# A decoder layer on one core: transposing x and x1 by VectorE blocks and DRAM instead of TensorE, and a new order for the first batch

## The chip, the cores and the metric

The kernel runs on one core of one Trainium2 chip. The metric is the device time of one execution in microseconds. The engines are called PE (TensorE), DVE (VectorE), ACT (ScalarE), POOL (GpSimd) and SP (SyncE, which here only issues DMAs). PEld is PE's weight load.

## The reference

There are 16 batches of 512 tokens with 256 channels, all in float32. One post-norm decoder layer is computed: a linear attention, a cross-attention on 64 context tokens per batch, and a mixture of 8 experts with a capacity of 1024 tokens each.

```python
x = layernorm(x + attn(x))          # q = x + x Wq + bq; two products of K^T V, 16 heads of 16
x = layernorm(x + xattn(x, ctx))    # 16 heads of 64, softmax over 64 context tokens
x = layernorm(x + ffn(x))           # router softmax, first 1024 tokens of each expert

# attn, for k in (0, 1):
states[k] = (x + x Wk[k] + bk[k])^T (x + x Wv[k] + bv[k])   # per head, scaled by 1/1024
out = q @ (states[0] * states[1])
out = layernorm(out) * ln_g + ln_b
out = out @ Wo + bo
```

Nearly all router weights are above zero, so each expert's first 1024 tokens are those of batches 0 and 1; the kernel works these two out beside the attention and has a loop at the end for whatever else would be routed.

## The kernel before

The self-attention never forms keys and values of tokens. For each batch it takes the Gram matrix of x (`gram`, L550 to L576: `gx` is x with a column of ones), and turns it with the weights into the state (`g_times_wk`, `states`) and into a 256 x 264 matrix `m`. The tokens then go through `m` (L687), a norm, the output projection (L711) and the norm that gives `x1`. A matmul contracts over partitions, so tokens that are to be multiplied have to lie with their channels on partitions. That is what `transposed` (L227 to L241) does: eight 128 x 128 transposes on PE (L233) into two PSUM banks, then one copy of each bank to SBUF. It is called for x (`xT`, L664), for x1 (`x1T`, L723), for the two batches of the experts and for weights and context in the setup. `zT` (L696 to L703) is transposed likewise and shares its buffer with `xT`. In `x1T` the tokens are put in another order (token 128 t + 32 q + i goes to column 32 t + i of block q), and its last row is set to one, so that the mask can be added as a row of the keys.

The cross-attention of a batch has four tiles of scores (L814), a softmax on DVE, ACT and POOL whose end is a transpose in blocks of 32 x 32 on DVE (`probsT`, L804), and then 256 matmuls in one go (L834) on the values already multiplied by the output weights (`vo`), which come from DRAM by SP's DMAs (L781). The experts' matmuls are L946 and L963.

The order of all instructions is settled when the program is built. Each part is a stream, a Python generator that yields between small steps. `Model` keeps an estimate of when each engine is free and each tile made; `weave` takes, of the streams that are ready, the one whose own clock is least. A stream's clock is `at + span * spent / total`, set by `plan`: how much of PE's time it has spent of its total, spread over its span. `yield WAIT` makes a stream wait until the estimate says that its last step is done, and `beside` runs a generator as a further stream. The setup is planned to last 115 us and each batch a STEP of 78 us. The plan of before has the self-attention of batch b from SETUP + (b - 1) STEP (L1071) and its cross-attention one STEP later (L1084); the experts are a stream over nearly the whole run (L1117). `in_order` then fixes the order on PE, DVE, ACT and POOL. Each engine works its list in order; all DMAs are issued from SP, in order too, and one that waits holds those behind it.

The lines that are spoken of: L186 and L188 (`evac`, copies on ACT and DVE in turn), L237 and L239 (the copies to `x1T`), L267 (a norm on ACT), L296 and L299 (`load_gram_x`: a memset on POOL and the load of `gx`), L426 (loads of context weights, `nat`), L611 (load of `xt`), L725 (POOL adds a bias to x1), L822 (exponentials), L870 (store of `x_rest`), L952 and L954 (relu of `hT`).

Of the kernel before, what the change touches and what calls it, by code (L numbers as in the profile page):

```python
# [18 lines left out]
P = 128  # L19
# [8 lines left out]
class Model:  # L28
# [37 lines left out]
    def run(self):  # L66
# [4 lines left out]
        for ins in traced[self.seen:]:  # L71
# [12 lines left out]
            if kind == "InstDMACopy":  # L84
# [13 lines left out]
            for n in names[0] + names[1]:  # L98
                self.used[n] = max(self.used.get(n, (0.0, None)), (done, engine), key=lambda p: p[0])
            for n in names[1]:  # L100
                self.made[n] = (done, engine)
# [15 lines left out]
def decoder_layer(  # L117
# [93 lines left out]

    not_last = const.tile([P, 1], FP, tag="not_last", name="not_last")
# [6 lines left out]
    w_sel = const.tile([P, NTT, E], FP, tag="w_sel", name="w_sel")  # L219
# [7 lines left out]
    def transposed(dst, src, view=lambda t: t, ones=False):  # L227


        for cc in range(NC):  # L230
# [4 lines left out]
            ps = ps if len(v.shape) == 2 else ps.rearrange("p (q t i) -> p q t i", q=NT, t=NT)  # L235
            if ones and cc == NC - 1:
                nc.vector.tensor_scalar(v, ps, not_last, ident[:, P - 1:P], ALU.mult, ALU.add)  # L237
            elif ones:
                nc.scalar.copy(v, ps)  # L239
            else:  # L240
                evac(v, ps)  # L241

# [29 lines left out]
    with ExitStack() as att:  # L272
# [20 lines left out]
        def load_gram_x(b, eng=nc.sync, pieces=1):  # L293
# [4 lines left out]
            for i in range(pieces):  # L298
                eng.dma_start(  # L299
                    out=t[:, i * n_:(i + 1) * n_, :C],  # L300
                    in_=x[b, i * n_ * P:(i + 1) * n_ * P, :].rearrange("(t p) c -> p t c", p=P),
                )
# [147 lines left out]
        def context_keys():  # L450
# [28 lines left out]
            last = small.tile([P, NP], FP, tag="last", name="last")  # L479
# [70 lines left out]
        def gram(b, u4):  # L550
# [12 lines left out]
            if b + 2 < B:  # L563
                gram_x[b + 2] = load_gram_x(b + 2)
# [10 lines left out]
            grams[b] = g  # L575
            yield WAIT  # L576
# [30 lines left out]
        grams, sums = {}, {}  # L607
# [6 lines left out]
        def self_attention(b, done):  # L614
# [4 lines left out]
            xT = wk1.tile([P, NC, S], FP, tag="xT", name="xT")  # L619
            gks = []  # L620
# [42 lines left out]
            yield from until(lambda: made(xt))  # L663
            transposed(xT, xt)  # L664
# [16 lines left out]
            yield WAIT  # L681
            z = wk1.tile([P, NT, CX], FP, tag="z", name="z")
            mm = moments()
            for t in range(NT):
                ps = bank("ps_o")
                for cc in range(NC):
                    nc.tensor.matmul(  # L687
                        ps[:, :CX], xT[:, cc, t * P:(t + 1) * P], m[:, cc, :], start=(cc == 0), stop=(cc == NC - 1)
# [19 lines left out]
            for t in range(NT):  # L708
# [7 lines left out]
                yield  # L716
            yield from until(lambda: finished["routing"] >= b - 1)
# [3 lines left out]
            x1T = wk2.tile([P, NC, S], FP, tag="x1T", name="x1T")  # L721

            transposed(x1T, x1, lambda t: t.rearrange("p (t q i) -> p q t i", q=NT, t=NT), ones=True)  # L723
            yield WAIT
            nc.gpsimd.tensor_add(x1, x1, cs["bout"].unsqueeze(1).to_broadcast([P, NT, CX]))  # L725
            done[b] = x1, x1T

# [37 lines left out]
        def cross_attention(b, x1, x1T):  # L765
# [41 lines left out]
            for t in range(NT):  # L807
# [3 lines left out]
                for hf in range(2):  # L811
                    ps = bank("ps_sim")
                    for cc in range(NC):
                        nc.tensor.matmul(  # L814
                            ps, x1T[:, cc, t * P:(t + 1) * P], kq[:, cc, hf * 512:(hf + 1) * 512],
# [59 lines left out]
        def ranks():  # L875
# [34 lines left out]
            nc.vector.scalar_tensor_tensor(w_sel, rank, float(CAP), w_all, ALU.is_lt, ALU.mult)  # L910
            NB = B - HEAD_B
            least = small.tile([P, NB], FP, tag="least", name="least")
# [9 lines left out]
        def last_norm(b, t):  # L922
            y = wk1.tile([P, C], FP, tag=("z", "xt")[t % 2], name="y")
# [120 lines left out]
        done, finished = {}, {"states": 0, "cross": 0, "routing": 0}  # L1044
# [24 lines left out]
        def all_self_attention():  # L1069
            for b in range(B):  # L1070
                self_st.plan(SETUP + (b - 1) * STEP, STEP, 16.5)  # L1071
                yield from until(lambda: b in grams and sums[b // QB][1] and "rb" in cs and made(grams[b], sums[b // QB][1][0]))
# [9 lines left out]
        def all_cross_attention():  # L1082
            for b in range(B):
                cross_st.plan(SETUP + b * STEP, STEP, 28.2 + (0 if b % GB else 4.0))  # L1084
# [33 lines left out]
        self_st.plan(0.0, SETUP, 16.5)  # L1118
        cross_st.plan(SETUP, STEP, 28.0)
# [40 lines left out]
    with tc.For_i(0, n, 1) as i:  # L1160
# [3 lines left out]
        nc.vector.tensor_copy(wb, w_sel[:, ds(i * NT + HEAD_B * NT, NT), :])  # L1164
# [47 lines left out]
```

## Time and profile before

| what | value |
|---|---|
| three runs | 1383.49, 1384.72, 1386.94 us, median 1384.72 |
| the profiled execution | 1389.4 us, of which its span is 1387.6 |
| busy: PE, DVE, ACT, POOL | 1365.9, 850.7, 402.2, 203.7 us |
| granted PE clock, mean | 0.994 |
| moved by DMA | 153.6 MB, 40.1% of 16 engines' span on SP's queue |
| groups of transposes at L233 | xt 128, x 128, nat 32, cn 16, x_head 16 |

The profile's page gives the busy time of each engine, the chain of waits that ended last, the groups of instructions with the mean length of one, and the DMA issues with the time from issue to landing. Of the further views, the windows give the busy time of each engine in a stretch, and the timeline gives the instructions with start, length and the idle time before them (in brackets, with what ended it). Times within the run are in us from the start of the span. Matmuls are pipelined, so the lengths of neighbours overlap, and the distance between starts is what one costs.

### The profile page before, as it was taken

Reading aid. Unit: us, or ns where it says so; the run is one execution under the profiler, and the core shown is the slowest. Engines: PE = TensorE matmul, PEld = TensorE weight load, DVE = VectorE, ACT = ScalarE, POOL = GpSimd, SP = SyncE. Lnnn points to the kernel's source line nnn. Section 1 sums busy time; section 2 is a strip of 40 time slices with the busy share of each in tenths; the row PEclk is TensorE's granted clock in tenths of the full one; section 3 lists DMA queues with packets and bytes.
Section 4 is the critical chain, followed back from the end, with each engine's and each line's share of the span. In section 5 each row is a group of like instructions: output and inputs, shape, how many; then the busy total and the mean of one; then the engine's idle time right before and its main releaser. Section 6 shows DMA issues by size and latency. Waiting matters only on the chain.

```text
span 1387.6 us, 24209 instructions
## 1 busy us (share of the span) xinstructions
PE 1365.9 (98%) x9630; PEld 1077.9 (78%) x9630; DVE 850.7 (61%) x1957; ACT 402.2 (29%) x912; POOL 203.7 (15%) x140
## 2 busy tenths in 40 slices
PE   8999999999999999999999999999999999999997
PEld 5766576877878787878878787878888787878686
DVE  2445848466584848475584848475665939484744
ACT  1134224132232314142233323142323323232322
POOL 0001112112020111112020112112020202111200
PEclk9999999999999999999999999999999999999999
DMA  8657775511515153522606053513334061505211
GB/s 260 203 136 191 189 195 163 142 32 42 145 53 150 46 142 106 127 77 52 181 24 164 31 142 106 126 62 77 110 95 123 16 187 46 147 26 126 91 56 40
DMA packets 98372, 153.57 MB, mean 111 GB/s; under 512 B 15560, under 2 KB 70096, under 8 KB 98256
## 3 DMA queue, kind: packets, MB, share of 16 engines
q1 hardware_dynamic: 98256, 151.98, 40.1%
q8 instruction: 78, 1.28, 0.4%
q14 instruction: 38, 0.31, 0.1%
HBM read 114.71 MB, written 37.22 MB: 109 GB/s over the span
## 4 chain that ended last, share of the span: by engine, by line
PE 89%; DVE 5%; DMA 2%; SPq 1%; ACT 1%; issue 1%; ACTq 0%; DVEq 0%
PE ps_x L834 16%; PE ps_sim L814 15%; PE ps_e L963 15%; PE ps_h L946 15%; PE ps_gk L629 4%; PE ps_p L711 4%; PE ps_o L687 3%; PE ps_kv L437 3%; PE ps_t L233 2%; PE ps_kq L751 2%; PE ps_vo L492 2%; PE ps_s L641 2%; PE ps_g L555 2%; PE ps_zt L700 1%; PE ps_m L670 1%; PE ps_g L560 1%
## 5 line engine op out<-in xcount | busy, mean ns | idle before, releaser
L946 PE MATMUL ps_h<-head_T,wi 128*128 128x256 f32 x1024 | 239.1, 379 | 0.0
L834 PE MATMUL ps_x<-vo,pT 32*128 32x264 f32 x4096 | 234.9, 384 | 3.9 <-DVE pT L804 3.7
L814 PE MATMUL ps_sim<-kq,x1T 128*128 128x512 f32 x512 | 235.0, 593 | 0.0
L834 PEld LDWEIGHTS ps_x<-vo,pT 32*128 32x128 f32 x4096 | 211.5, 186 | 26.1 <-issue 5.6
L946 PEld LDWEIGHTS ps_h<-head_T,wi 128*128 128x128 f32 x1024 | 193.4, 190 | 38.8 <-issue 13.0
L802 POOL TENSOR_TENSOR s<-s,sm 128x1024 f32<-128x1024 f32 x64 | 121.7, 1901 | 539.8 <-DVE sm L801 501.4
L841 DVE TENSOR_TENSOR x<-ps_x,x 128x264 f32<-128x264 f32 x64 | 23.2, 426 | 226.3 <-PE ps_x L834 226.3
L822 ACT ACTIVATE s<-s 128x512 f32<-128x512 f32 x128 | 80.7, 630 | 276.1 <-DVE s L821 276.0
L814 PEld LDWEIGHTS ps_sim<-kq,x1T 128*128 128x128 f32 x512 | 94.5, 190 | 83.2 <-issue 74.5
L820 DVE TENSOR_REDUCE mx<-ps_sim 128x8 f32<-128x512 f32 x128 | 86.1, 673 | 42.0 <-PE ps_sim L814 41.6
L821 DVE TENSOR_TENSOR s<-ps_sim,mx 128x512 f32<-128x512 f32 x128 | 88.5, 692 | 4.4
L725 POOL TENSOR_TENSOR x<-x,bout 128x1056 f32<-128x1056 f32 x16 | 38.7, 2420 | 320.7 <-ACT hT L952 172.6
L804 DVE STREAM_TRANSPOSE pT<-s 128x1024 f32<-128x1024 f32 x64 | 78.6, 1228 | 7.0 <-POOL s L802 7.0
L952 ACT ACTIVATE hT<-ps_h 128x256 f32<-128x256 f32 x128 | 46.9, 376 | 119.9 <-PE ps_h L946 119.8
L701 ACT ACTIVATE zT<-ps_zt,shift,gain 128x512 f32<-128x512 f32 x32 | 23.2, 775 | 189.5 <-PE ps_zt L700 189.5
L800 DVE TENSOR_REDUCE sm<-s 128x16 f32<-128x1024 f32 x64 | 77.1, 1204 | 0.4 <-ACT s L822 0.4
L261 ACT ACTIVATE rstd<-bn_mv,eps 128x4 f32<-128x4 f32 (+1 forms) x70 | 20.7, 295 | 159.5 <-DVE bn_mv L250 156.0
L267 ACT ACTIVATE x<-x,off,rstd 128x264 f32<-128x264 f32 (+1 forms) x112 | 58.3, 591 | 29.3 <-DVE off L265 29.3
L687 PE MATMUL ps_o<-m,xT 128*128 128x264 f32 x256 | 66.7, 387 | 0.0
L954 DVE TENSOR_SCALAR hT<-ps_h 128x256 f32<-128x256 f32 x128 | 52.2, 409 | 22.5 <-PE ps_h L946 22.3
L711 PE MATMUL ps_p<-wo,zT 128*128 128x264 f32 x256 | 63.1, 387 | 0.0
L629 PE MATMUL ps_gk<-wk,g 128*128 128x256 f32 x256 | 61.2, 382 | 0.0
(174 smaller groups left out, 1897.4 us busy)
## 6 DMA issues: line engine op xcount, KB each, us to landing
vo<-vo_dram SPq DMA_DIRECT2D x512, 132.0 KB, 4.2
vo_dram<-vst SPq DMA_DIRECT2D x128, 132.0 KB, 2.4
xt<-in_x_dram SPq DMA_DIRECT2D x16, 512.0 KB, 4.0
wi<-L_ffn_experts_inter_dram SPq DMA_DIRECT2D x8, 1024.0 KB, 5.3
gx<-in_x_dram SPq DMA_DIRECT2D x15, 512.0 KB, 4.2
x_rest<-x SPq DMA_DIRECT2D x14, 512.0 KB, 3.1
out_dram<-x SPq DMA_DIRECT2D x14, 512.0 KB, 2.9
kT<-k_dram SPq DMA_DIRECT2D x8, 512.0 KB, 3.3
```

Of the source, the lines that this page charges most:

```text
L629: nc.tensor.matmul(ps[:, :C], blk, wk[:, j, k, :], start=(j == 0), stop=(j == NC - 1))
L687: nc.tensor.matmul(ps[:, :CX], xT[:, cc, t * P:(t + 1) * P], m[:, cc, :], start=(cc == 0), stop=(cc == NC - 1))
L711: nc.tensor.matmul(ps[:, :CX], zT[:, cc, t * P:(t + 1) * P], wo[:, cc, :], start=(cc == 0), stop=(cc == NC - 1))
L802: nc.gpsimd.tensor_mul(s, s, sm.unsqueeze(2).to_broadcast([P, NH, J]))
L804: nc.vector.transpose(probsT[:, :, t, :], s.rearrange("p h (a j) -> p (h a) j", a=2))
L814: nc.tensor.matmul(ps, x1T[:, cc, t * P:(t + 1) * P], kq[:, cc, hf * 512:(hf + 1) * 512], start=(cc == 0), stop=(cc == NC - 1),)
L820: nc.vector.tensor_reduce(mx[:, hs], sim, AX.X, ALU.max)
L821: nc.vector.tensor_sub(s[:, hs, :], sim, mx[:, hs].unsqueeze(2).to_broadcast([P, 8, J]))
L822: nc.scalar.activation(s[:, hs, :], s[:, hs, :], AF.Exp, scale=SCALE)
L834: nc.tensor.matmul(ps[q][:, :CX], probsT[pq, blk].rearrange("p t i -> p (t i)"), vos[c][pq, i, :], start=(c == 0 and i == 0), stop=(c == 7 ...
L946: nc.tensor.matmul(ps[:, :TB], wi[:, cc, f * P:(f + 1) * P], head_T[b][:, cc, t0 * P:t0 * P + TB], start=(cc == 0), stop=(cc == NC - 1),)
L963: nc.tensor.matmul(ps[:, :C], hT[f][:, t * P:(t + 1) * P], wo_[:, f, :], start=(f == 0), stop=(f == NF - 1),)
```

## The change

For batches 1 to 15, x and x1 are transposed in two moves. DVE transposes blocks of 32 x 32 (`to_blocks`, four instructions of 128 x 256 elements), and the blocks then go to their partitions by way of DRAM: one store of 512 KB (`put_blocks`) and four loads of 128 KB (`from_blocks`), all issued from ACT. For x the blocks are made from `gx` after the Gram matrix; so that they come out in order, `gx` is loaded with 32 tokens to each partition group by four DMAs where there was one (the first batch's load is as before). The row of ones of x1T is made by a small activation on ACT ahead of the store. Batch 0 keeps `transposed`.

The part after the projection, from the norm of x1 to `x1T`, becomes a stream of its own (`scores_operand`), and the next self-attention no longer waits for it. The self-attention of batch b is planned from SETUP + (b - 1.6) STEP, 0.6 STEP earlier. The plan of batch 0's self- and cross-attention is zero, so they come first whenever they are ready. `xT` and `x1T` are laid out as blocks, the model gets a cost for DMAs issued from ACT, two small tiles get one buffer, and `w_sel` goes: its values are written over those of `w_all`.

```diff
+            if kind == "InstDMACopy" and engine == "Activation":
+                start = max(at, self.free.get(engine, 0.0))
+                self.free[engine] = start + 0.35
+                done = start + 5.0
...
+    taken = []
+
+    def to_blocks(src):
+        while taken:
+            yield 0.5
+        taken.append(src)
+        xb = wk1.tile([P, NT, NC, NT, 32], FP, tag="xb", name="xb")
+        for q in range(NT):
+            nc.vector.transpose(
+                xb[:, :, :, q, :].rearrange("p k c j -> p c k j"),
+                src[:, q, :C].rearrange("p (c k j) -> p c k j", c=NC, j=32),
+            )
+        yield WAIT
+        return xb
+
+    def put_blocks(name, xb):
+        there = dram.tile([NT, 32, NT, NC * P], FP, tag=name, name=name)
+        nc.scalar.dma_start(
+            out=there.rearrange("t i k n -> (t i) (k n)"), in_=xb.rearrange("p k c q j -> p (k c q j)")
+        )
+        taken.clear()
+        return there
+
+    def from_blocks(dst, there):
+        for k in range(NT):
+            nc.scalar.dma_start(
+                out=dst[k * 32:(k + 1) * 32].rearrange("i t c n -> i t (c n)"),
+                in_=there[:, :, k, :].rearrange("t i n -> i t n"),
+            )
...
-        def load_gram_x(b, eng=nc.sync, pieces=1):
+        def load_gram_x(b, eng=nc.sync, pieces=NT):
...
+                else:
+                    eng.dma_start(
+                        out=t[i * 32:(i + 1) * 32, :, :C],
+                        in_=x[b, i * P:(i + 1) * P, :].rearrange("(q j) c -> j q c", j=32),
+                    )
...
-            if b + 2 < B:
-                gram_x[b + 2] = load_gram_x(b + 2)
...
             grams[b] = g
+            if b > 0:
+                yield WAIT
+                xb = yield from to_blocks(gx)
+                x_blocks[b] = put_blocks(f"x_blocks{b}", xb)
+            if b + 2 < B:
+                gram_x[b + 2] = load_gram_x(b + 2)
             yield WAIT
...
+            if b > 0:
+                from_blocks(xT, x_blocks.pop(b))
...
-            yield from until(lambda: made(xt))
-            transposed(xT, xt)
+            if b == 0:
+                yield from until(lambda: made(xt))
+                transposed(xT.rearrange("p t c n -> p c t n"), xt, lambda t: t)
...
+            yield from until(lambda: made(xT))
             z = wk1.tile([P, NT, CX], FP, tag="z", name="z")
...
+            beside(self_st, scores_operand(b, xt, mm))
+
+        def scores_operand(b, xt, mm):
+
             yield from until(lambda: finished["routing"] >= b - 1)
             x1 = wk2.tile([P, NT, CX], FP, tag="x1", name="x1")
             yield from normalized(x1, lambda t: xt[:, t, :], mm=mm)
             yield WAIT
...
+                xb = yield from to_blocks(x1)
+
+                nc.scalar.activation(
+                    xb[:, NT - 1, NC - 1], xb[:, NT - 1, NC - 1], AF.Identity, bias=last_q[:, 0:1],
+                    scale=last_q[:, 1:2],
+                )
+                there = put_blocks(f"x1_blocks{b}", xb)
+                yield
+                yield from until(lambda: made(there))
+                from_blocks(x1T, there)
+                yield
+                yield from until(lambda: made(x1T))
             nc.gpsimd.tensor_add(x1, x1, cs["bout"].unsqueeze(1).to_broadcast([P, NT, CX]))
             done[b] = x1, x1T
...
-                self_st.plan(SETUP + (b - 1) * STEP, STEP, 16.5)
+                if b > 0:
+                    self_st.plan(SETUP + (b - 1.6) * STEP, STEP, 16.5)
...
-                cross_st.plan(SETUP + b * STEP, STEP, 28.2 + (0 if b % GB else 4.0))
+                if b > 0:
+                    cross_st.plan(SETUP + b * STEP, STEP, 28.2 + (0 if b % GB else 4.0))
...
-        self_st.plan(0.0, SETUP, 16.5)
-        cross_st.plan(SETUP, STEP, 28.0)
+        self_st.plan(0.0, 0.0, 1.0)
+        cross_st.plan(0.0, 0.0, 1.0)
```

## The prediction

> **What bounds the kernel now.** I read first the page's busy time and chain of waits, then the windows and TensorE's timeline, and last the lengths of the instructions concerned.
>
> ```profile
> span 1387.6 us, 24209 instructions
> ...
> PE 1365.9 (98%) x9630; PEld 1077.9 (78%) x9630; DVE 850.7 (61%) x1957; ACT 402.2 (29%) x912; POOL 203.7 (15%) x140
> ...
> PE 89%; DVE 5%; DMA 2%; SPq 1%; ACT 1%; issue 1%; ACTq 0%; DVEq 0%
> ```
>
> PE is idle for 1387.6 - 1365.9 = 21.7 us in all, and 89% of the chain that ends last is PE. So an instruction taken off PE comes off the end, unless another engine then makes PE wait. Where PE does wait shows in the windows (columns: PE, PEld, DVE, ACT, POOL busy, clock, DMA share, GB/s):
>
> ```profile
> 160.00:240.00 80.00, 77.63 (x546) 55.53 (x545) 53.90 (x118) 26.41 (x63) 15.27 (x11) 1.00 0.67 178
> 240.00:320.00 80.00, 79.51 (x608) 65.37 (x607) 47.41 (x106) 21.76 (x48) 11.32 (x8) 1.00 0.29 75
> 320.00:353.00 33.00, 29.75 (x322) 25.05 (x321) 15.86 (x34) 4.32 (x10) 6.76 (x5) 0.95 0.35 88
> ```
>
> That is 2.4 + 0.5 + 3.3 = 6.1 us. From 400 to 1300 us less than 1 us is idle; 6.1 us lie in the first 20 us (first loads) and 8.8 us after 1350 us (the last norms), which the change leaves alone. Then PE's timeline, for the price of one transposition and of one wait:
>
> ```profile
> 697.76 1.04 PE L233 MATMUL ps_t<-ident,xt 128*128 128x128 f32 x8
> 698.63 1.03 PE L946 MATMUL ps_h<-head_T,wi 128*128 128x256 f32 x4
> ```
> ```profile
> 329.87 3.70 PE L963 MATMUL ps_e<-wo__2016,hT 128*128 128x256 f32 x16
> 336.82 15.93 PE L834 MATMUL ps_x<-vo,pT 32*128 32x264 f32 x256 [3.25 <-DVE pT L804]
> ```
>
> Lengths overlap, so starts count: eight transposes hold PE for 698.63 - 697.76 = 0.87 us (the ones of x1 too: 679.43 to 680.30). The other pair shows that a wait costs more than itself: L834 takes 14.45 us as a rule, 15.93 here after 3.25 us of idleness.
>
> **What comes off PE.** For 15 of 16 batches both groups of L233, x's and x1's, go: 30 x 0.87 = **26.1 us**. In the full steps PE has nothing else missing, so all of it is on the path.
>
> **What VectorE gets.**
>
> ```profile
> L804 DVE STREAM_TRANSPOSE pT<-s x64: 1186/1233/1246, 155.8 to 1322.7; 128x1024 f32<-128x1024 f32 x64
> ```
> ```profile
> 685.50:724.40 38.90, 38.90 (x170) 28.38 (x170) 33.71 (x71) 10.45 (x23) 9.47 (x6) 1.00 0.11 40
> 724.40:738.90 14.50, 14.50 (x257) 13.07 (x258) 0.67 (x2) 2.07 (x4) 0.60 (x1) 1.00 0.75 195
> ```
>
> 1024 elements take 1233 ns; a transpose of 256 takes at least a quarter, 0.31, at most some 0.40 with a fixed part; I take 0.37. Eight a batch: 3.0 us. Gone are the copies of xT (0.68) and x1T (0.81). Net +1.5 us a batch, 22 us in all: 851 becomes 873 of 1360. The cover: VectorE is idle for most of the 14.5 us of L834. Without cover: in the stretch of the scores VectorE has 33.7 of 38.9 us, and L834 waits for its fourth pT; transposes that fall just before that pT cost up to 1.5 us a batch.
>
> Here a rule of the Trainium skill speaks against the change. VectorE: DVE Perf Modes, "Rules for kernel authors", gives a 128x128 transpose to TensorE where PSUM is an acceptable destination. The rows agree on the price alone: 0.87 us on PE against 4 x 0.37 = 1.5 on VectorE. By the rule nothing should move and the time stays 1385; by the windows PE is full and VectorE 61% busy, so the dearer engine is the cheaper place. I follow the windows.
>
> **What ScalarE gets.** Per batch ten DMA issues (one store and four loads, twice) and one small activation (0.35 from L822's 0.63 at four times the size); gone are two copies (0.57 + 0.59). An issue takes 0.38 to 0.54 us on SP (gx and vo). 10 x 0.45 + 0.35 - 1.15 = +3.7 us a batch, 55 us in all, 402 to about 457 us: hidden by 70% of idle ScalarE. Behind an issue that waits stand the relus of hT and the exponentials, which PE and VectorE want. Two places wait: x's loads wait until zT of the batch before, in the same buffer, has been used by L711, which PE reaches in the same order (1 to 2 us); x1's loads wait for their own store to land.
>
> ```profile
> gx<-in_x_dram SPq DMA_DIRECT2D x15, 512.0 KB, 4.2
> x_rest<-x SPq DMA_DIRECT2D x14, 512.0 KB, 3.1
> ```
>
> The nearest row for the store is x_rest, 3.1 us (2.8 to 4.4), and the planner places the loads 5.0 us after it. So ScalarE should rarely wait; I take +1 us for the whole run (bounds 0, as nothing can be gained here, and the rival's 37). Sharing the descriptor generator isn't in this trace, which has SP issues only[...]. If each issue on ScalarE waited for one of SP's, it would cost 2 x 0.54 and ScalarE 11 us a batch; still hidden.
>
> **What the transfers cost.** Each batch moves 2 x (0.5 + 0.5) MB more: 31 MB on 153.6, a DMA share of 40% to about 48%. The loads are 1 KB runs like gx's, 4.2 us for 512 KB. The rule against it: VectorE: DVE Perf Modes, "The three transpose paths", calls a plain DMA that transposes by strides 19 times slower than the DMA's own transpose, which it gives at 1.309 us for a 128x128 bf16 block. An estimate from that page: 512 KB are 16 such blocks by bytes, 16 x 1.309 x 19 = 398 us a transfer, five steps long, and the kernel would take many times longer. But its condition is a large innermost stride, and here VectorE has done the elements and DMA moves whole runs; I take gx's 4.2. Latency then is about 1.5 + 3 + 4 + issues, some 10 us in place of 2. x has its time from the Gram matrix to its use; x1's is met by starting self-attention 0.6 steps (47 us) earlier.
>
> **What is moved.** gx's next load and its memset on POOL go behind the block transposes; POOL then waits for VectorE where it waited for PE (236 us in all before, with nobody behind in need of it), free. gx is now loaded by four issues in place of one: three more on SP, 1.5 us a batch, against a queue that holds 17.4 us of vo issues a step; free in the steps. In the first 20 us it isn't:
>
> ```profile
> 4.09 0.51 SPq L299 DMA_DIRECT2D gx<-in_x_dram  x1
> ...
> 7.05 1.17 SPq L330 DMA_DIRECT2D bk_row<-in_L_attn_bk_dram  x2
> 8.81 0.38 SPq L426 DMA_DIRECT2D nat<-in_L_xattn_Wkv_dram  x1
> ```
>
> Three more issues of 0.5 us go ahead of nat, less the 0.6 us gap before it: nat comes 0.9 us later (0 to 1.5), and PE waits for nat there already (2.4 us). +0.9.
>
> Batch 0 first: self-attention and cross-attention of batch 0 run as soon as they can, so its scores no longer start at 142 us and L834 not at 188, and the experts, which fill PE beside the VectorE-heavy scores, can start before 228 us. At best it removes the 6.1 us of idleness at 160 to 353 us and the slow starts of the two long L834 (15.81 and 15.93 against 14.45), 2.8 more: -9. At worst its chain leaves as many new holes: +9. I take -2, since the work on PE is the same and only holes can change. The 2.8 us at half and 0.81 clock between 68 and 76 us may go or come with the order; counted in the bounds. Dropping w_sel and the two single buffers are for space: nothing.
>
> **The sum.** -26.1 + 1 + 0.9 - 2 = -26.2. The profiled execution took 1389.4 (span plus 1.8): 1363.2. The median of the runs shown is 4.7 lower: 1384.7 - 26.2 = **1358.5**.
>
> **The rivals.**
> 1. VectorE takes the place of the transposes: the +1.5 us a batch lies before the fourth pT and shows wholly, 15 x 1.5 = 23 us: 1381; by half, 1370. For: 33.7 of 38.9 us. Against: the planner counts VectorE's time and puts experts in the gap.
> 2. Slower: ScalarE stands at x1's loads. vo's issues begin 2.1 us into L834 and last 17.4 us, to 5 us after its end. A store caught behind them holds ScalarE until then, and zT (L701), which PE needs at once, is behind. PE has other work for at most some 2.5 us of these 5, so 2.5 us a batch: 15 x 2.5 = 37, 1396. It decides against the change from 26 / 15 = 1.7 us of PE stall a batch, that is, a store landing some 11 us after its issue (5.0 planned, plus five banks of 0.86 us that PE fills meanwhile, plus 1.7). Against it: x_rest lands within 4.4.
> 3. The order gives more than the holes taken here: holes and slow clock both go, -9 - 3 in place of -2: 1348.
> 4. That the change doesn't do what it says would be L233 still at 320 transposes; the code leaves no such way beyond batch 0.
>
> **Chances.** Forecast 0.60 (1350 to 1367); rival 1 0.19, of which about a quarter ends at no change; rival 2 0.14; rival 3 0.06; no change otherwise 0.01. The measurement tells 0.3% (4.2 us) from no change. Faster 0.60 + 0.14 + 0.06 = 0.80, same 0.06, slower 0.14. The range from 1347 to 1382 leaves out rival 2 and some of rival 3.
>
> **What will show it.** L233 with 80 transposes in place of 320; PE busy near 1340 with as little idleness; VectorE near 873 and new transposes of 0.31 to 0.40 us; stores of xb landing in 3 to 5 us and no relu or exponential waiting on one. It is wrong if PE's idle time grows by over 10 us: under VectorE's pT, rival 1; under hT or zT of ScalarE after a DMA, rival 2.

## The result and the profile after

The changed kernel takes 1403.86 us (median of 4 runs, 1399.02 to 1406.11), the kernel before 1385.83 beside it on the same chip: the ratio is 1.0127, 95% interval 1.0094 to 1.016. The change makes the kernel slower, by 18 us; the forecast was 26 us faster.

Lines have moved: scores L814 are now L895, values L834 L915, transposes L233 L241, relus L952 and L954 now L1037 and L1039; the block transposes are L266, the stores of blocks L275, their loads L283. The page of the changed kernel:

```profile
span 1404.4 us, 24085 instructions
...
PE 1353.5 (96%) x9390; PEld 1060.7 (76%) x9390; DVE 857.7 (61%) x2049; ACT 390.6 (28%) x897; POOL 203.8 (15%) x140
...
PE 77%; DVE 14%; DMA 4%; SPq 2%; ACT 2%; issue 1%; POOL 0%; ACTq 0%; DVEq 0%; POOLq 0%
```

PE is less busy, by 12.4 us, as intended, and yet the span is 16.8 longer: idle time went from 21.7 to 1404.4 - 1353.5 = 50.9 us. In the chain PE has 77% where it had 89, and DVE 14 where it had 5: DVE's work now stands between PE's. The groups of the transposes, by form:

```profile
L266 DVE STREAM_TRANSPOSE xb<-x 128x256 f32<-128x256 f32 x60 | 21.2, 409 | 3.8 <-DMA x_blocks<-xb 3.8
L266 DVE STREAM_TRANSPOSE xb<-gx 128x256 f32<-128x256 f32 x60 | 21.1, 408 | 0.0
```
```profile
L241 PE MATMUL ps_t<-ident,xt 128*128 128x128 f32 x8 | 2.0, 425 | 3.5 <-DMA xt<-in_x_dram 3.5
L241 PE MATMUL ps_t<-ident,x 128*128 128x128 f32 x8 | 1.1, 279 | 0.0
```

The change does what it says: x and x1 have 8 + 8 transposes left on PE (all forms together 80). A block transpose lasts 0.41 us, and since the four of a group overlap, a group holds DVE for 1.4 us: 42.3 us in all, 2.8 a batch. The transfers are as cheap as expected; each line of the page's DMA issues ends with the time to landing:

```profile
x_blocks<-xb ACTq DMA_DIRECT2D x30, 512.0 KB, 3.0
...
xT<-x_blocks ACTq DMA_DIRECT2D x60, 128.0 KB, 2.8
x1T<-x_blocks ACTq DMA_DIRECT2D x60, 128.0 KB, 2.9
```

So the operations themselves cost about what was said, and the end is still wrong by 44 us. The windows (PE, PEld, DVE, ACT, POOL busy, clock, DMA share, GB/s) show where:

```profile
0.00:160.00 160.00, 142.55 (x719) 96.88 (x723) 84.12 (x200) 43.55 (x94) 15.01 (x23) 0.97 0.65 178
160.00:240.00 80.00, 74.08 (x516) 53.60 (x508) 34.91 (x95) 21.59 (x55) 4.99 (x4) 0.94 0.84 217
240.00:320.00 80.00, 76.25 (x564) 60.30 (x565) 47.74 (x121) 21.57 (x51) 12.53 (x8) 0.98 0.54 147
320.00:400.00 80.00, 76.17 (x532) 61.66 (x531) 45.42 (x102) 19.86 (x44) 12.70 (x9) 0.98 0.40 111
```

PE is idle for 17.4 us by 160 us and for 13.5 between 160 and 400; before, 6.7 and 6.1. In the full steps, 400 to 1300 us, it is 12.2 where it was 0.4. With the rest (7.7, was 8.4) that is +29.2. The mean clock fell from 0.994 to 0.987: (1 - 0.987) x 1404.4 - (1 - 0.994) x 1387.6 = 9.9 us more of lost clock. With 22.2 us of PE's work gone (first experiment below) this adds up to about the 16.8 measured: -22.2 + 9.9 + 29.2 = +16.9. That it does so within 0.1 us is luck. The clocks are rounded, and busy time is not work alone: it holds short pauses between matmuls that follow each other slowly, which are worth some 6 us in one run below (e12).

What one such place looks like, in the timeline of the changed kernel in the step at 515 us:

```profile
515.22 1.23 DVE L885 STREAM_TRANSPOSE pT<-s 128x1024 f32<-128x1024 f32 x1
...
516.38 1.38 DVE L266 STREAM_TRANSPOSE xb<-x 128x256 f32<-128x256 f32 x4
...
519.32 1.90 POOL L883 TENSOR_TENSOR s<-s,sm 128x1024 f32<-128x1024 f32 x1 [5.15 <-DVE sm L882]
520.13 1.37 DVE L718 TENSOR_TENSOR state<-sk 128x256 f32<-128x256 f32 x1
521.18 2.59 POOL L805 TENSOR_TENSOR x<-x,bout 128x1056 f32<-128x1056 f32 x1
...
521.53 2.52 DVE L719 SCALAR_TENSOR_TENSOR state<-state,headmask 128x256 f32<-128x256 f32 x1
...
524.37 1.23 DVE L885 STREAM_TRANSPOSE pT<-s 128x1024 f32<-128x1024 f32 x1
...
525.65 1.17 PE L915 MATMUL ps_x<-vo,pT 32*128 32x264 f32 x16 [3.11 <-DVE pT L885]
```

Between the third pT and the fourth, DVE has block transposes of x1 (1.38 us) and work of the next self-attention, and PE then waits 3.11 us for the fourth pT. L718 and L719 take 1.37 and 2.52 us, and elsewhere 0.42: each ends 0.3 us after a POOL operation that ran when it began. Both have two inputs in SBUF. The Trainium skill (SBUF — State Buffer, "SBUF: two separate sides") says that such a DVE instruction and a POOL instruction that reads SBUF exclude each other for their whole length; these rows agree. So DVE loses 1.4 us here to the block transposes and (1.37 + 2.52 - 2 x 0.42) = 3.1 to the lock.

The lock isn't new with the change. In the kernel before, the small operation on `off` (L265, now L310; 62 of 128x4) takes 745 ns in the mean, now 351, while one on `w_all` (L860, now L941) went from 192 to 675. What changed is which operations meet POOL's, and whether the fourth pT stands behind them.

### The profile page after: what moved, and what is told of

Same layout as the page of the kernel before. It is cut to its first block, busy times and chain, and to the rows that moved or that the text cites. A ratio compares the mean times of both kernels' runs of the same rounds, so it can differ in the third digit from the quotient of the medians.

```text
span 1404.4 us, 24085 instructions
## 1 busy us (share of the span) xinstructions
PE 1353.5 (96%) x9390; PEld 1060.7 (76%) x9390; DVE 857.7 (61%) x2049; ACT 390.6 (28%) x897; POOL 203.8 (15%) x140
## 3 DMA queue, kind: packets, MB, share of 16 engines
q8 instruction: 76, 1.25, 0.4%
## 4 chain that ended last, share of the span: by engine, by line
PE 77%; DVE 14%; DMA 4%; SPq 2%; ACT 2%; issue 1%; POOL 0%; ACTq 0%; DVEq 0%; POOLq 0%
PE ps_x L915 16%; PE ps_e L1048 13%; PE ps_h L1031 12%; PE ps_sim L895 12%; PE ps_o L746 4%; PE ps_kv L489 3%; PE ps_gk L686 3%; PE ps_p L770 3%; PE ps_kq L832 2%; DVE sm L881 2%; DVE pT L885 2%; DVE s L902 2%; DVE mx L901 2%; PE ps_g L607 2%; DVE bn_st L294 1%; PE ps_s L698 1%
## 5 line engine op out<-in xcount | busy, mean ns | idle before, releaser
L915 PE MATMUL ps_x<-vo,pT 32*128 32x264 f32 x4096 | 241.5, 388 | 7.6 <-DVE pT L885 5.1
L915 PEld LDWEIGHTS ps_x<-vo,pT 32*128 32x128 f32 x4096 | 216.7, 188 | 30.8 <-DVE pT L885 6.4
L895 PE MATMUL ps_sim<-kq,x1T 128*128 128x512 f32 x512 | 238.1, 595 | 0.7 <-ACT vst L191 0.6
L895 PEld LDWEIGHTS ps_sim<-kq,x1T 128*128 128x128 f32 x512 | 96.0, 191 | 81.4 <-issue 71.4
L1037 ACT ACTIVATE hT<-ps_h 128x256 f32<-128x256 f32 x128 | 45.9, 373 | 156.4 <-PE ps_h L1031 135.2
L746 PEld LDWEIGHTS ps_o<-m,xT 128*128 128x128 f32 x256 | 48.7, 192 | 15.9 <-ACT m L732 5.3
L1039 DVE TENSOR_SCALAR hT<-ps_h 128x256 f32<-128x256 f32 x128 | 50.8, 404 | 16.1 <-PE ps_h L1031 16.1
L805 POOL TENSOR_TENSOR x<-x,bout 128x1056 f32<-128x1056 f32 x16 | 38.9, 2434 | 145.6 <-DVE xb L266 92.4
```

Of the source, the lines that this page charges most:

```text
L746: nc.tensor.matmul(ps[:, :CX], xT[:, t, cc], m[:, cc, :], start=(cc == 0), stop=(cc == NC - 1))
L895: nc.tensor.matmul(ps, x1T[:, t, cc], kq[:, cc, hf * 512:(hf + 1) * 512], start=(cc == 0), stop=(cc == NC - 1),)
L915: nc.tensor.matmul(ps[q][:, :CX], probsT[pq, blk].rearrange("p t i -> p (t i)"), vos[c][pq, i, :], start=(c == 0 and i == 0), stop=(c == 7 ...
```

## The experiments

All medians are of 4 to 14 runs; before, 1385.4 to 1387.4 us, ran beside each. "Idle" is PE's, from one profiled execution, which lies up to 6 us from the median; its stretches are 0 to 160, 160 to 400, 400 to 1300 us and the rest. "Hold" means that a self-attention waits until the x1 before it is normalised, as in the kernel before; without it the variants that put x1 back on PE would take xt too early.

| run | us | ratio (95%) | PE busy | idle: all = by stretch |
|---|---|---|---|---|
| before | 1386 | 1 | 1365.9 | 21.7 = 6.7 + 6.1 + 0.4 + 8.4 |
| the change | 1403.9 | 1.0127 (1.0094 to 1.016) | 1353.5 | 50.9 = 17.4 + 13.5 + 12.2 + 7.7 |
| e1 | 1395.1 | 1.0056 (1.0032 to 1.008) | 1351.8 | 47.0 = 16.4 + 10.6 + 12.3 + 7.7 |
| e2 | 1414.1 | 1.0193 (1.017 to 1.0216) | 1371.4 | 42.0 = 12.1 + 21.1 + 0.1 + 8.7 |
| e3 | 1401.0 | 1.0103 (1.0081 to 1.0125) | 1369.6 | 29.7 = 13.6 + 4.4 + 3.5 + 8.2 |
| e4 | 1373.0 | 0.9893 (0.9869 to 0.9918) | 1343.7 | 29.1 = 6.6 + 12.6 + 2.2 + 7.7 |
| e5 | 1405.2 | 1.0132 (1.0098 to 1.0165) | 1374.1 | 32.9 = 13.4 + 10.1 + 1.8 + 7.7 |
| e6 | 1437.1 | 1.0386 (1.0347 to 1.0426) | 1360.4 | 72.8 = 14.4 + 28.9 + 21.9 + 7.6 |
| e7 | 1406.6 | 1.0155 (1.0125 to 1.0185) | 1360.8 | 38.5 = 12.9 + 11.7 + 6.5 + 7.3 |
| e8 | 1408.4 | 1.0162 (1.0128 to 1.0196) | 1357.8 | 50.4 = 16.4 + 12.5 + 10.9 + 10.6 |
| e9 | 1410.3 | 1.0164 (1.0137 to 1.0191) | 1363.1 | 45.8 = 14.5 + 14.5 + 8.8 + 8.1 |
| e10 | 1392.4 | 1.0038 (1.0025 to 1.0052) | 1353.8 | 39.8 = 9.7 + 12.8 + 9.5 + 7.8 |
| e11 | 1399.8 | 1.0094 (1.0071 to 1.0118) | 1366.0 | 30.1 = 7.6 + 11.7 + 2.1 + 8.6 |
| e12 | 1405.1 | 1.0137 (1.0112 to 1.0163) | 1371.8 | 30.8 = 8.3 + 8.9 + 7.3 + 6.3 |
| e13 | 1392.8 | 1.0046 (1.0028 to 1.0064) | 1353.3 | 35.9 = 8.3 + 10.4 + 6.8 + 10.4 |
| e14 | 1386.6 | 0.9991 (0.9975 to 1.0007) | 1349.8 | 34.9 = 9.2 + 13.2 + 4.2 + 8.4 |
| e15 | 1393.5 | 1.0062 (1.0041 to 1.0083) | 1346.2 | 40.7 = 8.2 + 14.3 + 10.1 + 8.0 |
| e16 | 1398.0 | 1.0082 (1.0062 to 1.0101) | 1355.8 | 40.3 = 7.9 + 14.5 + 9.8 + 8.1 |
| e17 | 1399.6 | 1.009 (1.007 to 1.0111) | 1351.1 | 48.5 = 16.9 + 15.1 + 8.7 + 7.8 |
| e18 | 1436.7 | 1.0363 (1.0338 to 1.0387) | 1375.8 | 59.2 = 8.7 + 13.0 + 27.4 + 10.2 |

**What the transposes are worth: e4.** The kernel before, without the transposes of 15 batches and with nothing in their place.

```diff
-            transposed(xT, xt)
+            transposed(xT, xt, pe=b == 0)
```

> The kernel before, with the PE transposes of x and x1 left out for batches 1 to 15; the copies to xT and x1T stay but read x and x1 as they lie, so part of the computation is left out. It prices the PE term alone. If the term was right: 1386 - 26 = 1360. Theory C: above 1375.

The time, 1373.0 us, lies between the two that were expected. Busy time falls by 22.2 us (30 groups of 0.74, not 0.87; 0.78 if the 1.3 us that this run lost more to the clock, 0.993 against 0.994, are counted), the time by only 12.7: idle time grows by 7.4 though no engine got more to do. The weaver, which goes by PE's estimated work, had made another order, and the new waits lie at 160 to 400 us. That set the question for the rest: what is due to an order, and what to the blocks.

**The plan of batch 0: e1 and e2.** e1 is the change with batch 0 planned as before; e2 is the kernel before with the change's plan of batch 0 alone.

```diff
-                if b > 0:
-                    self_st.plan(SETUP + (b - 1.6) * STEP, STEP, 16.5)
+                self_st.plan(SETUP + (b - (1.6 if b else 1)) * STEP, STEP, 16.5)
...
-        self_st.plan(0.0, 0.0, 1.0)
-        cross_st.plan(0.0, 0.0, 1.0)
+        self_st.plan(0.0, SETUP, 16.5)
+        cross_st.plan(SETUP, STEP, 28.0)
```

> The changed kernel with one part undone: the self- and cross-attention of batch 0 get their old planned times back; the blocks by way of DRAM and the start 0.6 steps earlier stay. Theory A (the new order of the first batch costs: in the changed kernel PE has 10.8 us more idle time and some 7 us more of half clock before 260 us): about 1404 - 18 = 1386. Theory B (the cost lies in the steps, where VectorE and ScalarE now delay PE: 12 us of idle time from 400 to 1300 us that were not there): 1398 to 1404. Theory C (the transposes were never worth 26 us on PE): no change, 1404.

> The kernel before with only the new plan of batch 0; all transposes on PE, start of the others as before. Theory A: 1386 + 18 = 1404. Theory B and C: 1386, within 4.

Batch 0 first costs 28 us in the kernel before and 8.8 in the change (1403.9 to 1395.1). Neither theory fits both runs: e1 falls between its two times, and e2 is 10 us above the upper one. In e2 the first matmuls of the experts, which fill PE beside DVE's work, come at 240.2 us, behind 6.39 us of idleness, where before they came at 228.2; the values of batches 1 and 2 then wait for pT:

```profile
240.18 2.04 PE L946 MATMUL ps_h<-head_T,wi 128*128 128x256 f32 x4 [6.39 <-issue]
...
272.80 16.09 PE L834 MATMUL ps_x<-vo,pT 32*128 32x264 f32 x256 [6.75 <-DVE pT L804]
...
359.66 17.03 PE L834 MATMUL ps_x<-vo,pT 32*128 32x264 f32 x256 [5.49 <-DVE pT L804]
```

**Plan without blocks: e3 and e5.** All transposes are back on PE, with the hold. e3 has the change's plan, and gx still comes in four transfers; in e5 gx is one transfer and batch 0 is planned as before, so that the earlier start and the scores' stream stay.

```diff
-            if b > 0:
+            if False:
                 yield WAIT
                 xb = yield from to_blocks(gx)
...
-            if b == 0:
+            if True:
                 transposed(
...
+                yield from until(lambda: finished["x1"] >= b)
                 yield from self_attention(b, done)
```

> The changed kernel with all transposes back on PE: new plan of batch 0, start 0.6 steps earlier and the scores' operand as its own stream stay (the next self-attention is held until the norm of x1 is issued, so that xt isn't taken too early). Theory A and the variant that the earlier start costs: the blocks did give their 26 us, so 1404 + 26 = 1430. Theory B, the blocks themselves cost what they give back: 1386 to 1404.

> The changed kernel with every transposition back on TensorE (gx in one transfer), batch 0's plan as before, and self-attention held until the x1 before it is normalised. What stays of the change is the start of self-attention 0.6 steps earlier and the scores' operand as a stream of its own. Theory A (the loss lies in batch 0's plan and in the blocks' loads; the earlier start costs nothing): 1383 to 1389 us, idle time of TensorE near 22 us. Theory B (the earlier start puts VectorE's and GpSimd's work of self-attention into the stretch of the scores): 1391 to 1398, with 5 to 12 us more idle time between 400 and 1300 us, ended by VectorE.

Without a block anywhere these take 1401 and 1405 us. e3 lies where its theory B put it, and theory A of e5, by which the earlier start is free, falls. Theory B of e5 falls too: e5 is slower than it said, and the steps have 1.8 us of idle time, not 5 to 12. Two pairs have one plan each with and without blocks (beside the blocks, the hold differs in both and the transfers of gx in the second). From e3 to the change, busy falls by 16.1 and idle grows by 21.2; from e5 to e1, busy falls by 22.3 and idle grows by 14.1. Busy time on PE falls and waiting takes its place, in the first pair all of it. In time the blocks lose 2.9 us in the first pair (the intervals overlap) and gain 10.1 in the second (they do not).

**Blocks with the plan of before: e6 and e9; half of the blocks: e7 and e8.** e6 has all blocks, e9 those of x alone, both starting 1.0 steps ahead; e7 has x1 alone and e8 both from batch 4 on, starting 1.6 steps ahead. Batch 0 is planned as before in all four, with the hold.

```diff
-                if b > 0:
-                    self_st.plan(SETUP + (b - 1.6) * STEP, STEP, 16.5)
+                self_st.plan(SETUP + (b - 1) * STEP, STEP, 16.5)
```

> The blocks of the changed kernel for x and x1, but with the plan of before: self-attention starts 1.0 steps ahead, not 1.6, and batch 0 is planned as before (and the hold of the previous kernel). Theory B (the earlier start is what opens holes in the steps): 1372 to 1382 us, since the 13 to 22 us that TensorE gains remain and only the setup's extra loads cost. Theory A: no better than with batch 0's old plan alone, 1392 to 1398. A third, that x1's way through DRAM is too long for this start: over 1400, with L895 waiting for x1T.

> Only x goes by blocks, x1 stays on TensorE; batch 0 and the start of self-attention (1.0 steps ahead) as before. x has its time anyway, from the Gram matrix to its use, so no earlier start is needed. If the earlier start is the whole loss: half of the 22 us of TensorE's busy time comes through less the extra issues of gx in the setup, 1373 to 1380 us. If VectorE's block transposes or the loads cost by themselves: 1385 to 1395, with the new idle time ended by VectorE or by the loads of xT.

> Only x1 goes by blocks; x stays on TensorE and gx comes in one transfer; batch 0's plan as before, the 1.6 steps and the hold stay. Half of TensorE's saving (11 to 13 us) and half of the transfers. Setup as the reason: the first 160 us have their 7 us of idle time again, so 1383 to 1390. VectorE's work in the stretch of the scores as the reason: as costly as both, 1392 to 1398.

> Blocks for x and x1 from batch 4 on only; batches 0 to 3 on TensorE with gx in one transfer; batch 0's plan as before, the 1.6 steps and the hold stay. TensorE keeps 24 of 30 groups saved (about 18 of 22 us of busy time). Theory A (setup is what costs): idle time before 160 us back to about 7 and 1377 to 1386 us. Theory B (the steps cost): 1389 to 1396, with the idle time of 400 to 1300 us at 10 us or more.

e6 is the slowest of all, and its timeline holds a wait that the prediction hadn't seen:

```profile
217.60 1.39 DVE L266 STREAM_TRANSPOSE xb<-gx 128x256 f32<-128x256 f32 x4
...
238.17 1.42 DVE L266 STREAM_TRANSPOSE xb<-x 128x256 f32<-128x256 f32 x4 [17.50 <-DMA x_blocks<-xb]
```

x and x1 share one buffer of blocks. x's store stood on ACT behind four loads of xT, which took 5.36 us to issue, and a norm that ended at 228.7; it went out at 231.3 us only and took some 6.8 to land, and DVE, and PE behind it (12.80 us at 243, for state), stood until then. x1T's loads are issued at 252.2 us and the scores begin at 259.9, in the kernel before at 216.0. So a late x1 costs more than its latency, and with all blocks the earlier start is needed: e1, which has it, takes 1395.1 us and e6 1437.1. e9, which needs none, is no faster than the rest; e7, e8 and e9 all miss both of their forecasts to the slow side. In these four runs no part, undone alone, brings the time of before back.

**The weaving itself: e11 and e12.** e11 is a control, the change's code with every transposition on PE and both plans as before. e12 is the kernel before with one number changed:

```diff
-                self_st.plan(SETUP + (b - 1) * STEP, STEP, 16.5)
+                self_st.plan(SETUP + (b - 1) * STEP, STEP, 15.0)
```

> A control: every transposition on TensorE, both plans as before; of the change only the form stays, the scores' operand as a stream of its own (with self-attention held until the x1 before it is normalised, as in the other runs). If form and hold are neutral, 1383 to 1389 us, and the runs with the hold can be read as they stand. If another order of the same work costs by itself, above 1392.

> The kernel before with one number of the plan changed: self-attention is entered with 15.0 us of TensorE work a batch in place of 16.5, so that the streams are woven in another order; the work is the same. It measures what an order alone is worth. If the order of before is no better than others: 1382 to 1390 us. If any other order loses what the control lost: 1395 to 1402, with idle time at 160 to 400 us above 10.

The same work in another order costs 17.7 us in e12, as much as the change, and 13.0 in e11, where the scores' stream is new too; both lie at or above the upper of the times expected. The waits were expected at 160 to 400 us; in e12 they lie in the steps as well (7.3 us). (Written out, PE's list of some 1,000 groups differs from that of before in 475 lines for e11 and 554 for e12.) e12's places in PE's timeline:

```profile
258.48 11.76 PE L834 MATMUL ps_x<-vo,pT 32*128 32x264 f32 x176 [3.48 <-DVE off L265]
...
506.02 14.87 PE L834 MATMUL ps_x<-vo,pT 32*128 32x264 f32 x256 [0.79 <-DVE pT L804]
```

The fourth pT ends just too late in several steps, where in the kernel before it is just in time. Other short pauses don't show as idle time. In e12 PE is busy for 5.9 us more than before, with the same work and no lower clock (0.995); the transposes of z, which wait for z more often there, have 4.8 us more. Before, then e12:

```profile
L700 PE MATMUL ps_zt<-ident,z 128*128 128x128 f32 x128 | 17.4, 279 | 0.0
```
```profile
L700 PE MATMUL ps_zt<-ident,z 128*128 128x128 f32 x128 | 22.2, 287 | 6.9 <-ACT z L267 5.0 <-ACT vst L186 1.4
```

The kernel before is therefore no fair base for "the change minus its parts". It is the best of six orders with all transposes on PE; the other five (e2, e3, e5, e11, e12) take 1400 to 1414 us. The twelve versions with blocks that compute the whole layer take 1387 to 1437, half of them under 1400. None of these was drawn at random, so this doesn't show that blocks gain in an ordinary order; it shows that the two sets overlap.

**From batch 4 on only: e10, and what opens its holes: e13, e14, e15.** e10 has blocks and the earlier start from batch 4 on, the rest as before.

```diff
-            if b > 0:
+            if b >= QB:
                 yield WAIT
                 xb = yield from to_blocks(gx)
...
+                self_st.plan(SETUP + (b - (1.6 if b >= QB else 1)) * STEP, STEP, 16.5)
```

> Blocks for x and x1, and the earlier start of 1.6 steps, from batch 4 on only; batches 0 to 3 as before in everything. If what costs is the early start in the setup (waits for xt and the half clock after them): 400 us is reached as before and 24 groups saved remain, 1369 to 1378 us. If the steps themselves cost, idle time from 400 to 1300 us is 12 us or more and the time 1380 to 1388.

The first 160 us recover (9.7 us of idle), the steps don't (9.5), and the 1392.4 us lie above both forecasts. Two pairs of these runs differ in one number, the start of self-attention. From e8 to e10 batches 1 to 3 start 1.0 steps ahead in place of 1.6, with all their transposes on PE: 16.0 us faster, and the idle time before 160 us falls from 16.4 to 9.7. From e5 to e11 batches 1 to 15 do: 5.3 us faster (the intervals overlap). So the earlier start isn't free, through the order that it makes.

On this version, e13 leaves DVE's block transposes out, e14 issues the blocks' DMAs from SP, and e15 moves POOL's L805 behind the last softmax.

```diff
-        nc.scalar.dma_start(
+        nc.sync.dma_start(
             out=there.rearrange("t i k n -> (t i) (k n)"), in_=xb.rearrange("p k c q j -> p (k c q j)")
         )
```

> As the version with blocks from batch 4 on, but VectorE's block transposes and ScalarE's small activation are left out: x and x1 are stored as they lie and loaded by the same transfers (so scores and queries are computed from unpermuted elements). Stores, loads and ScalarE's issues stay. If VectorE's 3 us a batch open the holes of the steps: idle time from 400 to 1300 us falls from 9.5 to 4 or less, and 1383 to 1388 us. If the transfers and ScalarE's issues do: 8 us or more stay, 1389 to 1394.

> As the version with blocks from batch 4 on, but all stores and loads of blocks are issued by SP in place of ScalarE; the rest of the order is nearly the same. If ScalarE's issues (10 a batch) and waits open the holes of the steps: idle time from 400 to 1300 us falls by 3 to 6 us and 1384 to 1389 us. If not: 1389 to 1395. It may lose where a load waits on SP ahead of vo's.

> As the version with blocks from batch 4 on, but GpSimd's addition of bout to x1 stands behind the last softmax, right before the values' matmuls, in place of right behind x1's loads; every other order is unchanged. If this addition, running beside VectorE's work of the scores, is what stretches VectorE and delays the fourth pT: 2 to 5 us of idle time less from 160 to 1300 us, 1386 to 1390. If not: 1391 to 1395, no change.

e14 is the one that moves, as expected: 5.7 us faster than e10, in nearly the same order (41 lines of PE's list differ), the idle time of the steps down from 9.5 to 4.2. Two waits of e10 that are gone in e14:

```profile
764.84 3.56 PE L747 MATMUL ps_o<-m,xT 128*128 128x264 f32 x8 [2.31 <-DMA xT<-x_blocks]
...
1128.08 1.16 PE L729 MATMUL ps_m<-state,wqT 128*128 128x128 f32 x8 [2.59 <-DVE state L720]
```

e13 (another order again, 295 lines) takes 2.7 us of idle time out of the steps and no time off the whole; its time is the second of those expected, its idle time neither. e15, with PE's order unchanged, none: the addition at L805 isn't the one that matters in this order.

**Towards a faster version: e16, e17, e18.** e16 was built to keep the order of before on PE for its first 280 groups and starts blocks at batch 6, issued from SP; e17 is the whole change with its issues on SP; e18 is e14 with block transposes held back, where they can wait, until a step's last pT is done:

```diff
+            while pending:
+                pending.pop(0)()
             ps = [bank("ps_x") for _ in range(NT)]
```

> The order of before is kept instruction by instruction on TensorE for the first 280 groups (about 330 us); from batch 6 on x and x1 go by blocks, 1.6 steps ahead, with all block transfers issued by SP. 20 of 30 groups leave TensorE, by the run without transposes 0.74 us of busy time each: 15 us. If the loss of the change lies in the re-woven first 400 us and in ScalarE's issues: idle time before 400 us as in before (13 us), 3 to 6 us more in the steps, 1374 to 1381 us, faster than both kernels. If block work costs as much in the steps as it saves: 1384 to 1390.

> The whole change as it is, only its stores and loads of blocks issued by SP in place of ScalarE. Issues on ScalarE cost 5.7 us in the version with blocks from batch 4 on (23 to 24 transfers pairs of 30); here 4 to 8 us less than the change: 1396 to 1400. If SP's own queue then holds them up (vo's loads), no gain or a loss: 1402 or more.

> As the version with blocks from batch 4 on and issues on SP (1386.6 us), but VectorE's block transposes are held back until the last pT of a step is done, and stand right behind it, under the 14.5 us of the values' matmuls in which VectorE has nothing else: 16 of 24 groups of four come to lie there, the others, which can't wait that long, where they are ready. If block transposes ahead of the fourth pT are a main cost: the waits of 2.2 and 3.7 us before L917 at 259 and 345 us shrink and 1376 to 1383 us, faster than both kernels. If the order in general is what costs: 1384 to 1390, with other waits in their place.

e17 comes out as expected, 4.3 us below the change, though the intervals overlap; e16 and e18 are slower than both of the times expected of each. e16 is a close look at how an order that is nearly that of before loses time. The kernel before, ahead of the values at 252 us:

```profile
247.73 1.90 PE L555 MATMUL ps_g<-gx 128*128 128x257 f32 x8
...
249.47 1.05 PE L560 MATMUL ps_g<-gx 128*128 128x129 f32 x8
...
250.43 0.19 DVE L860 TENSOR_TENSOR w_all<-w_all,rm 128x32 f32<-128x32 f32 x1
...
250.79 2.35 POOL L705 TENSOR_TENSOR xt<-xt,bo 128x1024 f32<-128x1024 f32 x1
...
251.46 1.23 DVE L804 STREAM_TRANSPOSE pT<-s 128x1024 f32<-128x1024 f32 x1
...
252.74 1.62 PE L834 MATMUL ps_x<-vo,pT 32*128 32x264 f32 x24 [0.49 <-DVE pT L804]
```

and e16 at the same place:

```profile
250.18 3.62 PE L1055 MATMUL ps_e<-wo__2021,hT 128*128 128x256 f32 x16
...
252.69 2.34 POOL L767 TENSOR_TENSOR xt<-xt,bo 128x1024 f32<-128x1024 f32 x1
252.88 2.19 DVE L948 TENSOR_TENSOR w_all<-w_all,rm 128x32 f32<-128x32 f32 x1
255.00 1.41 DVE L266 STREAM_TRANSPOSE xb<-gx 128x256 f32<-128x256 f32 x4
256.34 1.20 DVE L892 STREAM_TRANSPOSE pT<-s 128x1024 f32<-128x1024 f32 x1
...
257.59 2.05 PE L922 MATMUL ps_x<-vo,pT 32*128 32x264 f32 x20 [3.79 <-DVE off L310]
```

Before, L860 ended 0.17 us ahead of POOL's addition; in e16 the same instruction begins 0.19 us after it and takes 2.19 us in place of 0.19. Block transposes (1.41) follow. So the fourth pT starts 10.8 us after the third (245.56 us) where it was 8.4 (243.11), 2.4 us later. PE's order isn't quite that of before either: the Gram matmuls (L555, L560) have left this place, the next such come at 306 us, and PE runs out of other work 0.9 us sooner, counted from the third pT. Together PE waits 3.79 us, where it waited 0.49.

e18 is nearly as slow as e6: x1T is late. (By the order that was planned, 16 of 24 groups of block transposes stand under the values; in the trace 13 begin there, as the values start or while they run.) Its scores wait 4.52 us for x1T's loads at 711 us and 2.41 at 905, and relus of the experts that were to fill the gap come late in turn (4.12 us at 1056, 4.14 at 1225).

## Why the prediction was wrong, by its steps

- **What comes off PE, -26.1.** The mechanism is right and the term too large: 22.2 us by e4, 0.74 us a group (0.78 with the clock) and not the 0.87 between two starts at one place. Wrong is "In the full steps PE has nothing else missing, so all of it is on the path". That held for the order before and not for the others made here; e4 shows it, with 12.7 of 22.2 us coming through.
- **What VectorE gets, hidden.** The price is right (2.8 us a batch, forecast 3.0), VectorE's total is not (857.7, forecast 873): its busy time contains waits for POOL, which change with the order (the 62 operations on `off` fell from 46.2 to 21.1 us). The cover was named rightly and not used: the transposes lie ahead of the fourth pT, rival 1, in the places shown. That all of them do isn't shown: the steps hold 12.2 us of idle time in all, and e13 got back 2.7 of 9.5.
- **What ScalarE gets, +1.** Too small: moving the issues to SP is worth 5.7 us for 24 of 30 groups in e14, and 4.3 for all 30 in e17, where the intervals overlap. (The 457 us of busy time couldn't show: the page counts no issue of a DMA as busy, and ACT stands at 390.6.) In the change it isn't rival 2 as written (a store caught behind vo's issues, 2.5 us a batch): stores land in 3.0 us, and DVE waits for the shared buffer of blocks for 3.8 us in all. A place where ACT's issues cost, in the changed kernel at 218 us:

```profile
212.65 8.92 SPq L549 DMA_DIRECT2D vo_dram<-vst  x14
...
218.34 3.43 ACTq L283 DMA_DIRECT2D x1T<-x_blocks  x4
...
221.81 0.59 ACT L732 COPY m<-ps_m 128x512 f32<-128x512 f32 x1 [3.11 <-DMA x1T<-x_blocks]
...
222.45 1.96 PE L746 MATMUL ps_o<-m,xT 128*128 128x264 f32 x5 [2.51 <-ACT m L732]
```

  From first to last the four issues take 3.43 us here, in turn with SP's, and 1.76 at 521 us, where SP issues nothing; the copy that PE needs stands behind them. That SP's issues are the reason isn't shown: each of the four takes 0.31 to 0.47 us by itself, the rest lies between them, and over the run ACT's issues beside one of SP's have the same median, 0.44 us, as the others. The bound for sharing of 11 us a batch was put down as hidden by ACT's idle time as a whole; what counts is the one instruction behind the issues.
- **The start, +0.9.** Too small. nat's first issue came at 11.02 us in place of 8.81, and its transposes start at 17.63 in place of 15.12. New waits of 1.15 (gx), 1.81 (weights) and 3.53 us (xt of batch 0, whose self-attention now comes first) follow: +10.7 us of idle time by 160 us, of which e3, with the same plan and loads of gx and no blocks, has 6.9. Batch 0's plan isn't the whole of it: e1, without it, has 16.4 us there to the change's 17.4.
- **What is moved: the earlier start, taken as free, and batch 0 first, -2 with bounds of 9 either way.** These are the steps that failed. Batch 0 first costs 8.8 us in the change, at the edge of the bounds, and 28 by itself, far outside; the experts, which were to start before 228 us, start at 262.6 in the change. The earlier start with the scores' stream costs 19.6 in e5. The start's own share depends on the order: 5.3 from e11 to e5, 16.0 from e10 to e8 for batches 1 to 3 alone; the stream without it costs 13 in e11, and e12 takes as long as the change with neither.
- **Missing from the sum: a new order.** An edit of a stream or of its planned work weaves all that follows anew, and the order of before was one in which the fourth pT, hT and zT come just in time, idle for 0.4 us in 900. The bounds on "holes" were taken from the 6 us visible before (the 8.8 us after 1350 us are 8.4, which has no bearing); e12 shows that an order alone can be worth 17.7. The forecast's own mark, wrong if PE's idle time grows by over 10 us, was met with 29.2.

The miss of the span, 16.8 + 26.2 = 43.0 us, is about 3.9 (the size of PE's term) + 29.2 (idle) + 9.9 (clock); the prediction had the clock's share only as up to 2.8 us, within its bounds. What stays open: how much of the 29.2 belongs to the blocks as such. Between equal plans they add 14 to 21 us of idle time, yet equal plans are not equal orders. And whether an order exists in which the change gains: the best tried, e14, is level with the kernel before (0.9991, 0.9975 to 1.0007), so no version here beats it.

## What to carry to other kernels

Where one engine is busy for 98% of the time in an order woven by estimates, work taken off it counts only if the next order is as tight: make a control first, the same work with one planning number changed, to see what an order alone can be worth. Ask of each operation that is moved onto an engine with time to spare which instruction there stands right ahead of the one that the full engine waits for; a free share of 39% covers nothing if the operation lands in front of the last pT. Issue DMAs from a queue that has nothing behind them that the full engine needs.

## What the runs showed of the hardware

A DVE operation of 0.19 us took 2.19, and one of 0.42 us took 2.52, when they began during a POOL operation of 1.9 to 2.6 us; the first took 0.19 in the kernel before, where it ended 0.17 us ahead of the same POOL operation. Four DMA issues on ACT took 1.76 us at one place and 3.43 at another, and whatever stood behind them on ACT waited as long.

A wait of PE can cost its clock as well. From 523.5 to 526.9 us, the stretch that ends with the 3.11 us wait for the fourth pT and the first matmuls behind it, the granted clock was 1.00; from 526.9 to 530.3 it was 0.50, with PE busy throughout; then 1.00 again. Over the run the clock made 9.9 us beside the 29.2 of idle time. The Trainium skill (TensorE: Matmul & The Clock Gate, "Part 1: The HAM clock gate") says that the clock halves after an idle window of about 3.4 us and recovers only after a busy one as long. The 3.4 us at half agree. The beginning doesn't quite: PE had been busy for 1.25 of the 3.4 us ahead of it, and in the kernel before the clock was 0.50 from 66.7 to 73.5 us with PE never idle. In the changed kernel it was 0.50 from 69.5 to 76.3 us, where the transposes of xt after 3.53 us of waiting took 425 ns each and those of x, elsewhere, 279. But that stretch is no longer than the one of the kernel before at 66.7 us, so it isn't what made the two kernels differ.
